# Causal attention on one core: each head's scores as two products of bfloat16 pieces, not three

## The chip, the cores and the metric

The kernel runs on one core of one Trainium2 chip. The metric is the device time of an execution in microseconds (us). TensorE (PE) multiplies matrices and writes its results to PSUM, a memory of eight banks here used in pieces of 128 partitions by 512 float32 numbers; VectorE (DVE) and ScalarE (ACT) read PSUM and SBUF; GpSimd (POOL) works on SBUF; SyncE (SP) issues most of the transfers. Each engine has its own queue, and semaphores hold an instruction until what it reads is there.

## The reference, cut to what matters

The program is a chain of four stages over one sequence of 2048 tokens of 128 features: a state-space layer, a layer of eight experts, causal attention with 16 heads of 8 features, and six layers of windowed attention with a gated network. Only the third is changed:

```python
scaling = D ** (-0.5)                       # D = 8
qkv = x @ W_qkv + b_qkv
q, k, v = jnp.split(qkv, 3, axis=-1)        # 16 heads each
scores = jnp.einsum('bhqd,bhkd->bhqk', q, k) * scaling
scores = jnp.where(mask[None, None, :, :], scores, -jnp.inf)    # causal
probs = jax.nn.softmax(scores, axis=-1)
out = jnp.einsum('bhqk,bhkd->bhqd', probs, v)
return out.transpose(0, 2, 1, 3).reshape(b, t, c) @ W_o + b_o
```

## The kernel before

**Pieces.** Scores are made by bfloat16 matmuls, and to keep nearly float32's precision, q and k are cut into bfloat16 pieces: the first piece is the rounded number, the next one the rounded rest, and so on. A head has 8 features, but its rows on TensorE are a strip of 32 partitions, in four slots of 8. Four heads form a group (`grp`, four groups), one strip each. The host lays out the weights (`_layouts`: `wqk`, `bqk`) so that the projection writes the same 8 features into the first three slots. The tile `kT` (`[P, NGRP, T]`) holds the first, second and third piece of k in those slots (`keys`), and constants of one in the first three rows of the fourth. The tile `q` (name `qT3`, `[P, 3, GW]`) holds one piece of q in each of its three planes, repeated over the slots (`project`). A product of plane i with kT is therefore one piece of q times all pieces of k; three products, summed in PSUM, make a score. Rows of the fourth slot of q's first plane take minus the row maximum, again in pieces, which the ones in kT add to each score.

**keys.** One call of the generator's step, for one group and 512 rows (a chunk `g`): PE projects into `pk`; ACT writes `one` (tile k0, shown as k) from it; DVE makes `krest`, the rest; POOL multiplies krest by a mask into `two` (tile k1, also shown as k) and subtracts it into kT. There are 16 calls: group 0 in `keys_values`, groups 1 to 3 in `keys`, for each of the four chunks. Buffers of one, two and krest rotate over two.

**project.** One call for each of 16 blocks (a group and 512 queries): PE projects into `pq`; ACT writes the first plane of q, DVE makes `qrest`, POOL casts it into the second plane and subtracts into the third. It is called a block ahead.

**Two passes.** For each block, `maxima` makes the scores with queries on the partitions and DVE takes their row maxima (`mx`, then `m`), which POOL splits (`m_piece`, `nm`) and PE transposes back (`ptm`) into the first plane of q. `attend` makes the scores again with keys on the partitions, ACT takes exp (`ex`), POOL zeroes the upper triangle of the diagonal tiles (an affine select on `ex`), and PE weighs the values (`av`). In the trace the products of maxima are sc<-kT,qT, those of attend sc<-qT,kT.

**The order.** Every instruction is pinned behind the one before it on its engine (`InOrder`), so the order of the program is that of each queue. `attention` interleaves the two passes: a unit of maxima (`part` of up to 512 keys, four heads) and a unit of attend (one tile of 128 keys, four heads) are taken together in two halves; each half has two heads of each pass:

```python
for half in range(2):
    m_heads, rest = step_m(ahead, half)
    heads, exps = part(1 - half)
    products(m_heads + heads)
    exps()
    weigh_due()
```

`products` runs over the pieces outside and the four heads inside, so that four strips of TensorE work at a time. `wanted` sets where units of one pass run alone. Scores and all other PSUM tiles of this stage take turns in seven banks (`psum_s`), the weighed values take the eighth.

**The beginning.** `front` gives each of the jobs (the end of the first stage, `experts`, `keys_values`, `keys`, and the attention's start) a due time, and `Merge` interleaves their steps by these times. Keys of the later chunks so stand among experts and halves of the attention: on ACT, for instance, after keys comes whatever step is due next, such as an exp.

Of the kernel before, what the change touches and what calls it, by code (L numbers as in the profile page):

```python
# [12 lines left out]
F32 = mybir.dt.float32  # L13
BF16 = mybir.dt.bfloat16
I32 = mybir.dt.int32
AF = mybir.ActivationFunctionType
ALU = mybir.AluOpType
# [3 lines left out]
P = 128  # L21
T = 2048
# [3 lines left out]
GW = G * P  # L26
# [6 lines left out]
HD1 = P // HEADS1  # L33
NGRP = 4
# [60 lines left out]
class Kernel:  # L95
# [102 lines left out]
    def load3(self, w):  # L198
        nc, a = self.nc, self.a
        wqk = w.tile([P, 2, NGRP, P], F32, name="wqk")  # L200
        nc.sync.dma_start(wqk, a["wqk1"])
        bqk = w.tile([P, 4, NGRP], F32, name="bqk")
        nc.sync.dma_start(bqk, a["bqk1"])
        wv = w.tile([P, P], F32, name="wv1")
        nc.sync.dma_start(wv, a["L1_attn_W_qkv"][:, 2 * P : 3 * P])
        wo = w.tile([P, P], F32, name="wo1")
        nc.sync.dma_start(wo, a["L1_attn_W_o"])
        self.w3 = wqk, bqk, wv, wo
# [259 lines left out]
    def keys(self, split, psum, g, hT3, kT, grps):  # L468
        wqk, bqk, wv, wo = self.w3
        hg = hT3[:, g * GW : (g + 1) * GW]  # L470
        for grp in grps:
            pk = psum.tile([P, GW], F32, name="pk", tag="b")
            self.pe.matmul(pk, lhsT=wqk[:, 1, grp, :], rhs=hg, start=True, stop=True)

            one, two = (split.tile([P, GW], BF16, name=f"k{i}") for i in range(2))
            rest = split.tile([P, GW], F32, name="krest")
            self.act.activation(
                one, pk, AF.Identity, bias=bqk[:, 2, grp : grp + 1], scale=bqk[:, 3, 0:1]
            )
            self.dve.scalar_tensor_tensor(rest, pk, bqk[:, 1, grp : grp + 1], one, ALU.add, ALU.subtract)  # L480
            self.gps.tensor_scalar_mul(two, rest, bqk[:, 3, 1:2])
            self.gps.tensor_tensor(kT[:, grp, g * GW : (g + 1) * GW], rest, two, ALU.subtract)
            yield 0.9

    def front(self, ctx, merge, psum, kvpool, x, hT3, kf, make_kT, va, xsT):
# [68 lines left out]
    def stages123(self, x, x3):  # L554
        nc, tc, a = self.nc, self.tc, self.a
        with ExitStack() as ctx:
            keep = ctx.enter_context(tc.tile_pool(name="s3keep", bufs=1))
            pool = ctx.enter_context(tc.tile_pool(name="s3", bufs=2))
# [3 lines left out]
            pe, dve, act, gps = self.pe, self.dve, self.act, self.gps  # L562
# [6 lines left out]
            wqk, bqk, wv, wo = self.w3  # L569
            hT = keep.tile([P, T], F32, name="hT3")  # L570
            kf = keep.tile([P, NGRP * T], F32, name="kf", tag="kT3")
            make_kT = lambda: keep.tile([P, NGRP, T], BF16, name="kT3", tag="kT3")
            va = keep.tile([P, NT, HEADS1, 32], F32, name="va")
            nms = [keep.tile([P, G, P], F32, name=f"nm{i}") for i in range(2)]
            xsT = keep.tile([P, T], F32, name="xsT", tag="ao")
# [2 lines left out]
            wait, kT = self.front(early, merge, banks, kvpool, x, hT, kf, make_kT, va, xsT)  # L578
# [23 lines left out]
            qs = {}  # L602
# [13 lines left out]

            def project(b):
                grp, qc = blocks[b]
                q = qs[b] = pool.tile([P, 3, GW], BF16, name="qT3", bufs=4)
                pq = bank("pq")  # L620
                pe.matmul(
                    pq, lhsT=wqk[:, 0, grp, :], rhs=hT[:, qc * GW : (qc + 1) * GW], start=True, stop=True
                )
                rest = pool.tile([P, GW], F32, name="qrest")
                act.activation(q[:, 0], pq, AF.Identity, bias=bqk[:, 0, grp : grp + 1])
                dve.scalar_tensor_tensor(rest, pq, bqk[:, 0, grp : grp + 1], q[:, 0], ALU.add, ALU.subtract)
                gps.tensor_copy(q[:, 1], rest)
                gps.tensor_tensor(q[:, 2], rest, q[:, 1], ALU.subtract)

            def products(heads):  # L630
                for i in range(3):
                    for product in heads:
                        product(i)


            def maxima(b):
                grp, qc = blocks[b]
                if b == 0:
                    project(b)
                q = qs[b]  # L640
                nm = nms[b % 2]
                m = pool.tile([P, G, 4], F32, name="m3")
                for j in range(G):
                    qt = G * qc + j
                    whole = (qt + 1) * P
                    chunks = [(c, min(GW, whole - c)) for c in range(0, whole, GW)]
                    mx = pool.tile([P, 4, NG], F32, name="mx3")

                    def part(pr, ch, qt=qt, mx=mx, chunks=chunks, j=j):
                        c, wd = chunks[ch]  # L650
                        n = len(chunks)
                        scs, heads = [], []
                        for h in (2 * pr, 2 * pr + 1):
                            sc = bank("sc1")
                            scs.append((h, sc))

                            def product(i, r=slice(32 * h, 32 * h + 32), sc=sc):
                                pe.matmul(
                                    sc[:, :wd], lhsT=q[r, i, j * P : (j + 1) * P], rhs=kT[r, grp, c : c + wd],
                                    start=i == 0, stop=i == 2 and ch < n - 1,  # L660
                                )

                            heads.append(product)

                        def rest():
                            for h, sc in scs:
                                if ch == n - 1:
                                    pe.matmul(sc[:, wd - P : wd], lhsT=self.ident16, rhs=mask, start=False, stop=True)
                                dve.reduce_max(mx[:, h, ch : ch + 1], sc[:, :wd], axis=AX.X)
                            if pr and ch == n - 1:  # L670
                                dve.tensor_reduce(m[:, j, :], mx[:, :, 0:n], axis=AX.X, op=ALU.max, negate=True)
                                if j == G - 1:
                                    pieces_of(m, nm)

                        return heads, rest

                    for ch, (_, wd) in enumerate(chunks):
                        yield wd, part, ch
                        if j == 0 and ch == 0 and b + 1 < len(blocks):
                            project(b + 1)  # L680

                def finish():
                    pt = bank("ptm")
                    for j in range(G):
                        pe.transpose(pt[:, j * P : (j + 1) * P], nm[:, j, :], self.ident)
                    dve.tensor_tensor(q[:, 0], q[:, 0], pt, ALU.add)

                yield 0, finish, None
# [14 lines left out]
            def attend(b):  # L703
                grp, qc = blocks[b]
# [14 lines left out]
                for kt in range(last + 1):  # L719
# [3 lines left out]
                    def part(pr, kt=kt, lo=lo):  # L723
                        nonlocal ex
                        if ex is None:
                            ex = pp.tile([P, 4, GW], F32, name="ex3")
                        scs, heads = [], []
                        for h in (2 * pr, 2 * pr + 1):
                            sc = bank("sc2")
                            scs.append((h, sc))  # L730

                            def product(i, r=slice(32 * h, 32 * h + 32), sc=sc):
                                pe.matmul(
                                    sc[:, lo:], lhsT=kT[r, grp, kt * P : (kt + 1) * P],
                                    rhs=q[r, i, lo:], start=i == 0, stop=i == 2,
                                )

                            heads.append(product)

                        def rest():  # L740
                            for h, sc in scs:
                                act.activation(ex[:, h, lo:], sc[:, lo:], AF.Exp)

                        return heads, rest
# [805 lines left out]
def _layouts(x):  # L1550

    f = np.float32
# [13 lines left out]
    got["bg"] = x["L0_ffn_bg"].reshape(1, P)  # L1566
    wqk = np.zeros((P, 2, NGRP, 4, 32), f)

    bqk = np.zeros((4, NGRP, 4, 32), f)
    for i in range(3):  # L1570
        s = slice(i * HD1, (i + 1) * HD1)
        wqk[..., s] = x["L1_attn_W_qkv"][:, : 2 * P].reshape(P, 2, NGRP, 4, HD1)
        bqk[0:2, ..., s] = x["L1_attn_b_qkv"][: 2 * P].reshape(2, NGRP, 4, HD1)
        if i:
            bqk[2, ..., s] = bqk[1, ..., s]
            bqk[3, 0, :, s] = 1.0
    bqk[3, 1, :, 2 * HD1 : 3 * HD1] = 1.0
    bqk[1, ..., 3 * HD1 : 3 * HD1 + 3] = 1.0
    got["wqk1"] = wqk.reshape(P, 2, NGRP, P)
    got["bqk1"] = bqk.reshape(4, NGRP, P).transpose(2, 0, 1)  # L1580
    got["bv1"] = x["L1_attn_b_qkv"][2 * P :].reshape(1, P)
    got["bo1"] = x["L1_attn_b_o"].reshape(1, P)
    swap = lambda s: np.concatenate([s[:, HD // 2 :], s[:, : HD // 2]], axis=1)
# [32 lines left out]
```

## Time and profile before

| | us |
|---|---|
| median of 3 runs (2319.01 to 2319.07) | 2319.02 |
| profiled execution | 2321.57 |
| its span, first to last instruction | 2319.6 |
| changed part: first keys to last scores | about 141 to 785 |

The profile is of one execution. A row of a group gives line, engine, operation, tiles (out<-in), shapes and count, then busy time, mean ns of one instruction, idle time of the engine before them and what ended it. A row of the timeline or of the chain of waits starts with the start in us and the duration. Every operation of this kernel is issued by one line of a helper (L67), so tiles and not lines tell them apart. The chain of waits follows the work that ended last back from the end, at each step to what released it.

### The profile page before, as it was taken

The numbers are of one execution on the slowest core, as the hardware profiler recorded it, in microseconds if no ns is written. First come the engines' busy times: TensorE is split into PE (matmuls) and PEld (weight loads), VectorE is DVE, ScalarE is ACT, GpSimd is POOL, SyncE is SP. The second block draws the span as 40 slices with busy tenths as digits, with TensorE's granted clock in tenths as the row PEclk, the third lists the DMA queues.
The fourth block names the chain that finished last, engine by engine and source line by source line (L and its number), as shares of the span: only waits on it lengthen the run. The fifth ranks groups of instructions, "written<-read, shape, count | busy, mean of one in ns | idle before, by whom it ended". The sixth has DMA issues, their size and how long they took to land.

```text
span 2319.6 us, 62002 instructions
## 1 busy us (share of the span) xinstructions
PE 2128.0 (92%) x26188; PEld 1233.9 (53%) x26188; DVE 1874.4 (81%) x2808; ACT 1638.1 (71%) x3219; POOL 1391.5 (60%) x2122
## 2 busy tenths in 40 slices
PE   4777988999999779999999999999999999999997
PEld 2654323333333346666666666666666666666654
DVE  6667677777766489999899988998999899998963
ACT  3322445566656578888888888888888888888881
POOL 4235411100011489988788878887888887887850
PEclk8787989999999979999999999999999999999998
DMA  2000000000000100000000000000000000000000
GB/s 78 1 1 1 2 2 2 2 2 2 2 2 2 68 2 20 4 20 2 20 11 23 2 20 11 22 2 20 11 22 2 20 9 3 2 2 2 2 6 14
DMA packets 14135, 25.38 MB, mean 11 GB/s; under 512 B 1657, under 2 KB 10530, under 8 KB 13090
## 3 DMA queue, kind: packets, MB, share of 16 engines
q1 hardware_dynamic: 13276, 20.97, 2.8%
q8 instruction: 206, 3.38, 0.6%
q14 instruction: 71, 0.58, 0.1%
q10 hardware_dynamic: 582, 0.46, 0.1%
HBM read 20.37 MB, written 1.05 MB: 9 GB/s over the span
## 4 chain that ended last, share of the span: by engine, by line
PE 64%; DVE 19%; ACT 8%; issue 4%; POOL 3%; DMA 0%; DVEq 0%; POOLq 0%; ACTq 0%; SPq 0%
PE big L67 45%; PE sc L67 9%; PE av L67 5%; DVE mx L67 4%; DVE rot_a L67 3%; DVE rot_b L67 2%; ACT sq L67 2%; ACT L67 1%; ACT ge L67 1%; DVE at L67 1%; ACT zs L67 1%; PE py L67 1%; ACT ex L67 1%; DVE act L67 1%; DVE ss L67 1%
## 5 line engine op out<-in xcount | busy, mean ns | idle before, releaser
L67 ACT ACTIVATE sm<-sm,mx,rn 128x64 f32<-128x64 f32 x1536 | 519.2, 430 | 0.3
L67 DVE TENSOR_REDUCE mx<-sc 128x1 f32<-128x512 f32 (+3 forms) x640 | 355.0, 604 | 125.5 <-PE sc L67 118.6
L67 POOL TENSOR_TENSOR rot_a<-rot_a,rot_b 128x1024 f32<-128x1024 f32 x192 | 454.6, 2368 | 0.1
L67 ACT ACTIVATE ex<-sc 128x512 f32<-128x512 f32 (+3 forms) x640 | 302.6, 536 | 204.1 <-PE sc L67 200.8
L67 PE MATMUL big<-wqk,s 128*128 128x512 f32 x768 | 369.2, 604 | 15.0 <-DVE rot_b L67 10.2
L67 PE MATMUL big<-zs,vo 128*128 128x256 f32 x1536 | 366.9, 382 | 0.3 <-ACT zs L67 0.3
L67 PEld LDWEIGHTS big<-zs,vo 128*128 128x128 f32 x1536 | 280.6, 190 | 88.3 <-issue 56.8
L67 DVE TENSOR_TENSOR rot_a<-big,tab 128x1024 f32<-128x1024 f32 x192 | 233.5, 1216 | 47.1 <-ACT sq L67 36.4
L67 PE MATMUL sc<-qT,kT 32*128 32x512 bf16 (+3 forms) x1920 | 248.4, 351 | 24.6 <-DVE mx L67 16.3
L67 ACT ACTIVATE sq<-big 128x1024 f32<-128x1024 f32 x192 | 197.4, 1028 | 76.0 <-PE big L67 46.1
L67 ACT COPY zs<-big 128x1024 f32<-128x1024 f32 x192 | 192.3, 1006 | 64.3 <-PE big L67 64.3
L67 PE MATMUL sc<-kT,qT 32*128 32x512 bf16 (+3 forms) x1920 | 232.4, 359 | 1.6 <-DVE krest L67 0.5
L67 DVE TENSOR_REDUCE ss<-sq 128x16 f32<-128x1024 f32 x192 | 229.8, 1198 | 1.4
L67 DVE TENSOR_TENSOR rot_b<-big,tab 128x1024 f32<-128x1024 f32 x192 | 230.0, 1198 | 0.3 <-POOL rot_a L67 0.3
L67 PE MATMUL big<-at,xw 32*128 32x512 f32 x1536 | 206.2, 624 | 3.9 <-DVE rot_b L67 1.7
L67 PEld LDWEIGHTS big<-wqk,s 128*128 128x128 f32 x768 | 135.7, 192 | 137.0 <-issue 125.6
L67 PE MATMUL big<-ident,rot_a 128*128 128x128 f32 x1536 | 198.9, 276 | 6.2 <-POOL rot_a L67 3.6
L67 PEld LDWEIGHTS big<-ident,rot_a 128*128 128x128 f32 x1536 | 176.6, 142 | 50.3 <-issue 23.5
L67 POOL TENSOR_SCALAR_AFFINE_SELECT ex<-ex 128x512 f32<-128x512 f32 x64 | 40.8, 638 | 269.8 <-ACT ex L67 269.6
L67 POOL TENSOR_TENSOR sm<-sm,su 128x1024 f32<-128x1024 f32 x96 | 183.1, 1907 | 23.4 <-DVE su L67 22.2
L67 PE MATMUL av<-ex,va 128*32 128x256 f32 (+1 forms) x2432 | 180.5, 377 | 5.0 <-POOL ex L67 3.7
L67 POOL TENSOR_TENSOR rot_a<-rot_a,rn 128x1024 f32<-128x1024 f32 x96 | 182.7, 1904 | 0.2
(236 smaller groups left out, 3342.4 us busy)
## 6 DMA issues: line engine op xcount, KB each, us to landing
wqk<-in_L_ffn_Wqkv SPq DMA_DIRECT2D x12, 512.0 KB, 4.9
wvo<-in_wvo SPq DMA_DIRECT2D x6, 1024.0 KB, 4.9
w<-in_L_ffn_W SPq DMA_DIRECT2D x6, 341.0 KB, 7.5
x<-in_L_attn_hidden_states SPq DMA_DIRECT2D x4, 256.0 KB, 4.3
out<-act SPq DMA_DIRECT2D x4, 256.0 KB, 2.3
rot<-in_rot SPq DMA_DIRECT2D x1, 960.0 KB, 7.0
w<-in_L_ffn_W SPq DMA_DIRECT2D x12, 64.0 KB, 1.9
qks<-in_qks SPq DMA_DIRECT2D x6, 128.0 KB
```

Of the source, the lines that this page charges most:

```text
L67: return self._tc.keep_in_program_order(call(*args, **kw))
```

## The change

q now has two planes and kT two. Plane 1 of kT is the old kT (three pieces of k in three slots) but with k's first piece in the fourth slot instead of the constants of one; plane 0 is made from it by one more ACT instruction that multiplies by a mask (first three slots) and adds a bias (the ones in the fourth slot). Plane 0 of q is q's first piece in three slots, made by one more ACT instruction from a tile `one`; plane 1 holds q's second piece in three slots and its third piece in the fourth, made on POOL: a multiply by a mask into `two` and a subtraction. The products with index 0 and 1 then contain what the three contained, but for the third piece of q, which meets only the first piece of k.

```diff
     def load3(self, w):
-        bqk = w.tile([P, 4, NGRP], F32, name="bqk")
+        bqk = w.tile([P, 5, NGRP], F32, name="bqk")
     def keys(self, split, psum, g, hT3, kT, grps):
             self.dve.scalar_tensor_tensor(rest, pk, bqk[:, 1, grp : grp + 1], one, ALU.add, ALU.subtract)
             self.gps.tensor_scalar_mul(two, rest, bqk[:, 3, 1:2])
-            self.gps.tensor_tensor(kT[:, grp, g * GW : (g + 1) * GW], rest, two, ALU.subtract)
+            cols = slice(g * GW, (g + 1) * GW)
+            self.gps.tensor_tensor(kT[:, 1, grp, cols], rest, two, ALU.subtract)
+            self.act.activation(
+                kT[:, 0, grp, cols], kT[:, 1, grp, cols], AF.Identity, bias=bqk[:, 3, 3:4], scale=bqk[:, 3, 2:3]
+            )
             yield 0.9
     def stages123(self, x, x3):
-            make_kT = lambda: keep.tile([P, NGRP, T], BF16, name="kT3", tag="kT3")
+            make_kT = lambda: keep.tile([P, 2, NGRP, T], BF16, name="kT3", tag="kT3")
             def project(b):
-                q = qs[b] = pool.tile([P, 3, GW], BF16, name="qT3", bufs=4)
+                q = qs[b] = pool.tile([P, 2, GW], BF16, name="qT3", bufs=4)
...
-                act.activation(q[:, 0], pq, AF.Identity, bias=bqk[:, 0, grp : grp + 1])
-                dve.scalar_tensor_tensor(rest, pq, bqk[:, 0, grp : grp + 1], q[:, 0], ALU.add, ALU.subtract)
-                gps.tensor_copy(q[:, 1], rest)
-                gps.tensor_tensor(q[:, 2], rest, q[:, 1], ALU.subtract)
+                one, two = (pool.tile([P, GW], BF16, name=f"q{i}") for i in range(2))
+                act.activation(one, pq, AF.Identity, bias=bqk[:, 0, grp : grp + 1])
+                dve.scalar_tensor_tensor(rest, pq, bqk[:, 0, grp : grp + 1], one, ALU.add, ALU.subtract)
+                act.activation(q[:, 0], one, AF.Copy, scale=bqk[:, 3, 2:3])
+                gps.tensor_scalar_mul(two, rest, bqk[:, 4, 0:1])
+                gps.tensor_tensor(q[:, 1], rest, two, ALU.subtract)
             def products(heads):
-                for i in range(3):
+                for i in range(2):
                     for product in heads:
                         product(i)
```

In both passes the product of index i now takes plane i of kT (`kT[r, i, grp, ...]` in place of `kT[r, grp, ...]`) and the last index is 1 and not 2. The host's layout fills the fourth slot of `wqk` and `bqk` too, and adds the masks: row 3 of `bqk` gets entries 2 (first three slots) and 3 (ones of the fourth), row 4 a mask of the fourth slot.

More of the change, by code (lines that the diff above doesn't have):

```diff
@@ L658, in product @@
                                 pe.matmul(
-                                    sc[:, :wd], lhsT=q[r, i, j * P : (j + 1) * P], rhs=kT[r, grp, c : c + wd],
-                                    start=i == 0, stop=i == 2 and ch < n - 1,
+                                    sc[:, :wd], lhsT=q[r, i, j * P : (j + 1) * P], rhs=kT[r, i, grp, c : c + wd],
+                                    start=i == 0, stop=i == 1 and ch < n - 1,
                                 )
@@ L733, in product @@
                                 pe.matmul(
-                                    sc[:, lo:], lhsT=kT[r, grp, kt * P : (kt + 1) * P],
-                                    rhs=q[r, i, lo:], start=i == 0, stop=i == 2,
+                                    sc[:, lo:], lhsT=kT[r, i, grp, kt * P : (kt + 1) * P],
+                                    rhs=q[r, i, lo:], start=i == 0, stop=i == 1,
                                 )
@@ L1567, in _layouts @@
     wqk = np.zeros((P, 2, NGRP, 4, 32), f)
-    bqk = np.zeros((4, NGRP, 4, 32), f)
-    for i in range(3):
+    bqk = np.zeros((5, NGRP, 4, 32), f)
+    for i in range(4):
         s = slice(i * HD1, (i + 1) * HD1)
@@ L1573, in _layouts @@
         bqk[0:2, ..., s] = x["L1_attn_b_qkv"][: 2 * P].reshape(2, NGRP, 4, HD1)
-        if i:
+        if i in (1, 2):
             bqk[2, ..., s] = bqk[1, ..., s]
@@ L1577, in _layouts @@
     bqk[3, 1, :, 2 * HD1 : 3 * HD1] = 1.0
-    bqk[1, ..., 3 * HD1 : 3 * HD1 + 3] = 1.0
+    bqk[3, 2, :, : 3 * HD1] = 1.0
+    bqk[3, 3, :, 3 * HD1 : 3 * HD1 + 3] = 1.0
+    bqk[4, 0, :, 3 * HD1 :] = 1.0
     got["wqk1"] = wqk.reshape(P, 2, NGRP, P)
-    got["bqk1"] = bqk.reshape(4, NGRP, P).transpose(2, 0, 1)
+    got["bqk1"] = bqk.reshape(5, NGRP, P).transpose(2, 0, 1)
     got["bv1"] = x["L1_attn_b_qkv"][2 * P :].reshape(1, P)
```

## The prediction

> **What bounds the kernel now.** I read the page first, then the busy time by windows over the third stage (the changed code runs from 135 to 785 us), then the timeline of some of its halves, the chain of waits through its beginning, and the groups by shape. A measurement here can tell about 0.2%, some 4.6 us, from no change; "same" means within that.
>
> ```profile
> PE 2128.0 (92%) x26188; PEld 1233.9 (53%) x26188; DVE 1874.4 (81%) x2808; ACT 1638.1 (71%) x3219; POOL 1391.5 (60%) x2122
> 135.00:300.00 165.00, 135.30 (x1237) 71.17 (x1236) 112.38 (x273) 57.41 (x133) 77.97 (x99) 0.86 0.00 1
> 300.00:785.00 485.00, 440.78 (x5768) 158.75 (x5769) 335.15 (x653) 288.33 (x596) 63.58 (x143) 0.97 0.02 6
> ```
> The window rows give, after the length, PE, PEld, DVE, ACT and POOL, then the granted clock. From 300 on PE is busy for 441 of 485 us, DVE for 335, ACT for 288: TensorE leads, VectorE is not far behind. Before 300 nothing is full; order and latency decide. In both parts the engines take the order in which the program names its instructions.
>
> ```profile
> 559.73 0.23 PE L67 MATMUL sc<-kT,qT 32*128 32x128 bf16 x2
> 560.49 0.64 PE L67 MATMUL av<-ex,va 128*32 128x256 f32 x8
> 566.57 0.39 PE L67 MATMUL sc<-kT,qT 32*128 32x512 bf16 x2
> 566.79 0.38 PE L67 MATMUL sc<-kT,qT 32*128 32x512 bf16 x2
> 567.01 0.38 PE L67 MATMUL sc<-kT,qT 32*128 32x512 bf16 x2
> 567.38 0.64 PE L67 MATMUL av<-ex,va 128*32 128x256 f32 x8
> 567.42 2.68 DVE L67 TENSOR_REDUCE mx<-sc 128x1 f32<-128x512 f32 x4 [0.23 <-PE sc L67]
> 568.90 0.64 PE L67 MATMUL av<-ex,va 128*32 128x256 f32 x8
> 570.29 0.64 PE L67 MATMUL av<-ex,va 128*32 128x256 f32 x8
> ```
> This timeline is the unit of the stage, a half: twelve products (three rounds of four heads), then eight weighing matmuls (av). Rounds follow each other at 0.22 us (566.57, 566.79, 567.01). A half without a wait goes from first product to first av in 0.76 us (559.73 to 560.49). From 567.38 to 570.29 two halves take 2.91 us while four reductions keep DVE for 2.68 of it, idle for 0.23 before them: here DVE is nearly the bound.
>
> ```profile
> 141.03 0.75 ACT k L67
> 141.81 0.77 DVE krest L67
> 142.67 1.58 POOL k L67
> 144.32 1.15 POOL kT L67
> 145.48 1.56 POOL k L67
> 147.11 1.16 POOL kT L67
> 148.30 0.75 DVE krest L67
> 149.05 1.20 DVE own L67 x2
> ```
> This is the chain of waits through the keys of the first 512 rows. Four keys calls (one for each group of heads) follow each other there, and the chain runs through them: POOL hands out one kT each 2.79 us (142.67 to 145.46 or 145.48), and behind the last krest (148.30) stand the experts' instructions on DVE (own). The chain runs likewise through the keys at 169 to 176, 198, 209 to 219, 237 and 257 to 261 us.
>
> **The products removed.** Each head's score goes from three products to two, one round of 0.22 us per half. By the code's schedule 126 units carry a maximum part and an attend part (two halves each), 34 a maximum part alone and 34 an attend part alone (one pass of four heads each). The widest head of every half and pass sums to 152,448 columns; at 0.215 us per 512 that is 64 us, the end of the range if TensorE alone set the pace. The other end is near zero: the reductions stay, and 448 of them are 512 wide.
> I go by the bursts of products after 300 us, from first product to what PE does next: 77 take 0.70 to 0.765 us (no wait), 20 less (narrow), 78 take 0.77 to 1.0, 76 longer (134.9 us in all), those mostly waiting for DVE. The first gain the whole round, 77 x 0.215 = 16.6 us; the narrow ones 20 x 0.1 = 2. The third kind falls to DVE's pace, (2.91 - 2.68)/2 = 0.11 us each: 78 x 0.11 = 8.6. Of the last I give a quarter of a round, 76 x 0.05 = 4, since a run of reductions that already fills DVE ends when it ends. With 3 us for the part before 300: **34 us gained**, bounds 18 and 50.
>
> **The projection of q.** Each of 16 calls gets one more ACT instruction (q[:, 0] from one) and a POOL multiply by a per-partition mask in place of the cast.
> ```profile
> L67 POOL TENSOR_SCALAR k<-krest,bqk 128x512 bf16<-128x512 f32 x16 | 25.1, 1567 | 21.6 <-DVE krest L67 21.6
> L67 POOL CAST qT<-qrest 128x512 bf16<-128x512 f32 x16 | 9.8, 612 | 41.5 <-DVE qrest L67 41.2 <-PE sc L67 0.3
> ```
> The same form of multiply takes 1567 ns in keys, the cast 612: +0.955 us on POOL, in front of the masks of the diagonal scores (ex, affine select). Those already arrive late: at 552.86 PE waits 0.41 us for POOL ex, directly behind the projection's two instructions. In about eight of the 16 calls a mask follows directly: 8 x 0.955 = **8 us lost**; bounds 0 (all covered) and 16 x 0.955 = 15. The extra ACT step waits for nothing that is late; ACT is busy for 59% after 300 and I count it at nothing; uncovered it costs 16 x 0.7 = 11.
> The Trainium skill, "GPSIMD Engine Reference", Engine selection, calls one-input work on this engine roughly line-rate, which would make both instructions alike and this term 0, and the total 8 us lower; the two rows above, 1567 and 612 ns on the same shape, speak against that.
>
> **The keys, where I expect the loss.** kT now has two planes. POOL writes plane 1; then ACT makes plane 0 from it, in the same step of the program. No row shows an ACT operation on bf16 from SBUF of this size; nearest are kT<-kT,carry (128x256, SBUF, 511 ns) and k<-pk,bqk (128x512, 779 ns): bounds 0.51 and 0.78, I take 0.7, nearer the second for its width. What counts is the wait. ACT's order is fixed, so the new instruction holds ACT until POOL is done, and behind it stands the next keys call's first instruction (k), for which DVE's krest waits, for which all of DVE's queue waits. One keys call then follows the other at 0.78 (k) + 0.75 (krest) + 1.57 + 1.15 (POOL) + 0.7 + some 0.35 for the five hand-overs (0.03 to 0.1 each in the chain) = 5.3 us, not 2.79.
> - Keys at 141 to 148: first krest 141.81, fourth now 148.30, then 141.81 + 3 x 5.3 = 157.7: **+9.4**. What is late next: own, then py on PE, both on the chain.
> - Keys at 169 to 176: likewise 169.05 + 15.9 against 175.52: **+9.4**.
> - Keys at 198 (one call): ACT's next work is at 205.62, after 8.46 us idle, and the new step would end at about 202: nothing.
> - Keys at 209 to 216 (three calls, between halves of the attention): the exps of two halves (2.16 us) stand between the second and third k, so krest moves from 215.89 to 209.49 + 10.6 + 2.2, and the scores' seven PSUM banks stay taken until the exps have run: 6 to 9, I take **8**.
> - One call at 235: the four exps behind it move from 235.84 to the end of kT and the new step, 240.6; seven banks let PE run on for a while: **3** (0 to 5).
> - Keys at 256 to 261 (three calls, a q projection between): the third krest moves from about 261.5 to 257.11 + 10.6 + 2.7 for q's longer steps, and the exps at 261.01 come behind all three, at about 274: 9 to 13, I take **12**.
> Sum **42 us lost**. If half of it were covered, 21; with every exp waiting, 50.
>
> **The clock.** While ACT waits, PE runs dry. In the trace the granted clock is already 0.86 over 135 to 300, and the same pair of pk matmuls takes 1.08 us at 213.90 and 2.07 at 254.19. I add two such doublings, **2 us** (0 to 10).
> The skill's "TensorE: Matmul & The Clock Gate", Part 1, says that an idle window of about 3.4 us halves TensorE's clock and that as long a busy one is needed to restore it; estimated from that page, some nine new gaps would cost up to 1.7 us each, 15 us instead of 2, and the total would be 13 us higher.
>
> The rest has one answer: the longer bqk load (20 instead of 16 numbers per partition) lies under the load of x; q's buffers shrink and one and two take their place; kT's planes fill the space kf leaves. 0.
>
> **Sum.** -34 + 8 + 42 + 2 = +18 us. The profiled execution took 2321.57 us (span 2319.6 and 1.97 around it), 2.55 over the median of the runs; so 2339.6 by its own time, and 2337 as a median.
>
> **Rivals.**
> - The keys' waits are covered, and it gets faster. If merged work lets DVE and PE run on while ACT waits, the front costs little and -34 + 8 = -26 remains: 2293. For it: PE idles 30 of 165 us there, so work is at hand. Against it: the chain runs through krest at each of these places, and the queues don't change order. It decides from 26 us, a mean wait of 1.9 us more per call over 14 calls. Chance 0.19.
> - DVE becomes the bound throughout: the rounds save only 16 us, q's longer POOL steps cost 15, the rest stays: -16 + 15 + 42 + 2 = +43, 2362. For it: the 76 bursts that already wait. Against it: DVE idles 150 of 485 us. Chance 0.2.
> - The shorter bursts bring nothing because something else paces a half: the third round would then vanish without av coming earlier. The spacing of 0.22 in rows of unhindered halves speaks against it; with it +52, 2371. Chance 0.04.
> My forecast, a front loss over the gain, has the rest, 0.57; its own range is 2318 to 2355.
>
> **Range and chances.** 2300 to 2362 leaves out most of the first rival and the last. Faster by over 0.2%: the first rival and a little of the forecast, 0.21; within 0.2%: the forecast's low end, 0.10; slower 0.69.
>
> **What would show it.** Right: ACT idle before kT with POOL kT as releaser, over 35 us in 16 waits; the first sc products some 19 us later than 190.6; unhindered halves at 0.54 us; in the steady blocks (affine selects at 499.8, 552.2 and 604.5 now, 52.4 us apart) a spacing of 48 to 50; POOL's q multiply at 1.57. Wrong: kT waits under 1 us, or krest still paced by POOL, or a block spacing under 46.5.

## The result and the profile after

The kernel after takes 2325.75 us (median of 12 runs, 2323.39 to 2329.88) where the kernel before, run beside it, takes 2319.05: the ratio is 1.0025, 95% interval 1.0016 to 1.0034, so some 6 us slower. The forecast was slower, by 18. The profiled execution of after took 2329.88 us (span 2328.0), 8.3 over that of before.

Placed by landmarks of the two traces: the seventh projection of q (pq6), which stands just behind the last key of the front, starts at 285.55 us before and at 327.05 after, 41.5 later. The last ex ends at 781.51 and at 791.73, so 31.3 of that were regained in the attention. The rest of the program gave 1.8 more, so the traces show 8.5 us; the profiled executions lie 4.1 (after) and 2.5 (before) above their medians, which differ by 6.7. A small sum of two large terms, then, as forecast; one of the two was mis-sized.

The page's engine line, and two of its groups:

```profile
PE 2092.3 (90%) x24908; PEld 1199.1 (52%) x24908; DVE 1865.9 (80%) x2808; ACT 1660.2 (71%) x3251; POOL 1403.7 (60%) x2122
...
L67 DVE TENSOR_REDUCE mx<-sc 128x1 f32<-128x512 f32 (+3 forms) x640 | 348.9, 604 | 111.5 <-PE sc L67 110.5
...
L67 PE MATMUL av<-ex,va 128*32 128x256 f32 (+1 forms) x2432 | 187.5, 390 | 11.5 <-POOL ex L67 9.9
```

PE has 1280 instructions fewer and ACT 32 more, as the diff says. The same two groups on the page of before:

```profile
L67 DVE TENSOR_REDUCE mx<-sc 128x1 f32<-128x512 f32 (+3 forms) x640 | 355.0, 604 | 125.5 <-PE sc L67 118.6
...
L67 PE MATMUL av<-ex,va 128*32 128x256 f32 (+1 forms) x2432 | 180.5, 377 | 5.0 <-POOL ex L67 3.7
```

The row of av is the price on POOL: before, av waited 3.7 us for the masked ex, now 9.9. The row of mx shows that DVE still idles 110 us for scores, 119 before.

The busy time by windows over the front and the attention of after (length, PE, PEld, DVE, ACT, POOL, granted clock):

```profile
135.00:300.00 165.00, 105.43 (x677) 55.21 (x680) 82.30 (x210) 51.60 (x105) 74.47 (x82) 0.74 0.00 1
327.00:795.00 468.00, 412.45 (x4836) 132.68 (x4835) 339.38 (x679) 303.34 (x624) 75.10 (x146) 0.93 0.02 6
```

In the same first 165 us PE now does 677 matmuls where it did 1237, at a clock of 0.74 where it had 0.86. No engine there is busier than before; that the order makes it late is shown below (x1_plane_later).

The front, in the waits of after from 135 to 330 us (who waited for whom; us in all, times, longest), and in the chain through the first keys:

```profile
ACT kT L67 <- POOL kT L67: 63.5, 16, 5.1
...
DVE krest L67 <- ACT k L67: 40.8, 13, 5.9
...
POOL k L67 <- DVE krest L67: 37.5, 12, 7.8
```

```profile
140.80 0.76 DVE krest L67
...
141.66 1.58 POOL k L67
...
143.32 1.16 POOL kT L67
...
144.50 0.81 ACT kT L67
145.31 0.67 ACT k L67
...
146.01 0.76 DVE krest L67
```

The first list is a ring: ACT waits for POOL's kT, DVE for ACT's k, POOL for DVE's krest. The chain goes round it once per key: krest at 140.80 and again at 146.01, 5.2 us later (forecast 5.3; 2.79 before).

In the attention, the steady blocks. These are POOL's masks on the timeline of after:

```profile
527.39 1.23 POOL L67 TENSOR_SCALAR_AFFINE_SELECT ex<-ex 128x512 f32<-128x512 f32 x2
...
576.02 1.22 POOL L67 TENSOR_SCALAR_AFFINE_SELECT ex<-ex 128x512 f32<-128x512 f32 x2
...
625.20 1.23 POOL L67 TENSOR_SCALAR_AFFINE_SELECT ex<-ex 128x512 f32<-128x512 f32 x2
```

They are 48.6 and 49.2 apart, inside the 48 to 50 of the forecast. Some long bursts shrank by more than one round, though. The same burst of twelve products before (545.18) and of eight after (568.17), each in its timeline:

```profile
545.18 0.39 PE L67 MATMUL sc<-kT,qT 32*128 32x512 bf16 x2
...
545.32 2.67 DVE L67 TENSOR_REDUCE mx<-sc 128x1 f32<-128x512 f32 x4
...
546.05 0.32 PE L67 MATMUL sc<-qT,kT 32*128 32x384 bf16 x1 [0.48 <-DVE mx L67]
...
546.63 0.64 PE L67 MATMUL av<-ex,va 128*32 128x256 f32 x8
```

```profile
568.17 0.39 PE L67 MATMUL sc<-kT,qT 32*128 32x512 bf16 x2
...
568.62 0.34 PE L67 MATMUL sc<-qT,kT 32*128 32x384 bf16 x2
...
568.88 0.64 PE L67 MATMUL av<-ex,va 128*32 128x256 f32 x8
```

From first product to av it took 1.45 us and now takes 0.71: 0.74 saved by leaving out a round of 0.22. The other half microsecond is the wait for DVE (0.48 at 546.05), which is gone. Elsewhere it isn't. At 481.24 before and at 509.66 after, again in one and the same burst, the wait has grown by what the round took:

```profile
481.24 0.37 PE L67 MATMUL sc<-qT,kT 32*128 32x512 bf16 x1 [0.21 <-DVE mx L67]
```

```profile
509.66 0.37 PE L67 MATMUL sc<-qT,kT 32*128 32x512 bf16 x1 [0.42 <-DVE mx L67]
```

Both times this burst takes 1.33 us.

### The profile page after: what moved, and what is told of

Read it like the earlier page. It is cut to its first block, busy times and chain, and to the rows that moved or that the text cites. A ratio compares the mean times of both kernels' runs of the same rounds, so it can differ in the third digit from the quotient of the medians.

```text
span 2328.0 us, 59452 instructions
## 1 busy us (share of the span) xinstructions
PE 2092.3 (90%) x24908; PEld 1199.1 (52%) x24908; DVE 1865.9 (80%) x2808; ACT 1660.2 (71%) x3251; POOL 1403.7 (60%) x2122
## 4 chain that ended last, share of the span: by engine, by line
PE 60%; DVE 20%; ACT 9%; issue 5%; POOL 5%; DMA 0%; DVEq 0%; POOLq 0%; ACTq 0%; SPq 0%
PE big L67 44%; PE sc L67 6%; DVE mx L67 5%; PE av L67 5%; DVE rot_a L67 3%; DVE rot_b L67 2%; ACT sq L67 2%; ACT ex L67 1%; ACT L67 1%; ACT ge L67 1%; DVE at L67 1%; PE py L67 1%; ACT zs L67 1%; DVE ss L67 1%; DVE act L67 1%
## 5 line engine op out<-in xcount | busy, mean ns | idle before, releaser
L67 DVE TENSOR_REDUCE mx<-sc 128x1 f32<-128x512 f32 (+3 forms) x640 | 348.9, 604 | 111.5 <-PE sc L67 110.5
L67 PE MATMUL sc<-qT,kT 32*128 32x512 bf16 (+3 forms) x1280 | 205.3, 372 | 36.8 <-DVE mx L67 15.5
L67 PE MATMUL av<-ex,va 128*32 128x256 f32 (+1 forms) x2432 | 187.5, 390 | 11.5 <-POOL ex L67 9.9
L67 PE MATMUL sc<-kT,qT 32*128 32x512 bf16 (+3 forms) x1280 | 190.0, 375 | 5.8 <-DVE krest L67 1.8
```

Source lines behind the costliest of these rows:

```text
L67: return self._tc.keep_in_program_order(call(*args, **kw))
```

## The experiments

My theory: the front costs some 42 us because ACT waits at the head of its order; the rounds save more than I gave them; q's longer POOL step costs what I gave it or more. The rivals: POOL's own chain sets the front's pace; DVE bounds the gain; POOL's step is covered. All times are medians, all ratios against the kernel before run on the same chip, with 95% intervals. To compare kernels measured at different times I multiply differences of ratios by 2319 us; such a difference carries about 3 to 5 us of uncertainty.

### Each part alone

The rounds alone, from the kernel before:

```diff
-                for i in range(3):
+                for i in range(2):
                     for product in heads:
```

(with `stop` at index 1.) Expected:

> The kernel before with two rounds of score products in place of three: the product of the third piece of q is left out, so the scores are less exact; the third piece is still made. It is the gain of the change by itself. Theory (bursts measured in the two traces, 47 us shorter after pq6 with the change): 38 to 50 us faster than before, 2269 to 2281. My forecast's term: 31 to 34 faster, 2285 to 2288. Rival (DVE's maxima bound the attention, the products are hidden beside them): under 20 us faster, over 2299.

Measured: 2278.02 us, ratio 0.9827 (0.9813 to 0.984), so 40 us faster, as the bursts of the trace said. From pq6 to the last ex its trace takes 448.8 us, before 496.0. DVE doesn't bound the gain as that rival had it; with the same reductions to make, it now idles less for scores than the 118.6 us of before:

```profile
L67 DVE TENSOR_REDUCE mx<-sc 128x1 f32<-128x512 f32 (+3 forms) x640 | 348.1, 602 | 90.7 <-PE sc L67 89.9
```

The keys' extra ACT step alone, from the kernel before:

```diff
-            self.gps.tensor_tensor(kT[:, grp, g * GW : (g + 1) * GW], rest, two, ALU.subtract)
+            cols = slice(g * GW, (g + 1) * GW)
+            self.gps.tensor_tensor(kT[:, 1, grp, cols], rest, two, ALU.subtract)
+            self.act.activation(
+                kT[:, 0, grp, cols], kT[:, 1, grp, cols], AF.Identity, bias=bqk[:, 3, 1:2], scale=bqk[:, 3, 0:1]
+            )
```

> The kernel before with the front's part of the change alone: POOL's last step writes plane 1 of a kT of two planes, ACT writes plane 0 from it in the same place of its order as in the kernel after, and nobody reads plane 0; three rounds and q's steps as before. It is the price of the wait by itself. Theory: 35 to 45 us slower than before, 2354 to 2364, with pq6 near 327 (before 285.6). Rival (the front of the kernel after is late for its colder clock or for something that q's steps bring): under 15 us slower.

Measured: 2364.61 us, ratio 1.0202 (1.0189 to 1.0215), 47 us slower, a little over the range. pq6 starts at 329.43, and the attention behind it takes 496.5 us, as before: the whole loss of the trace lies in the front. The wait in its list:

```profile
ACT kT L67 <- POOL kT L67: 62.2, 16, 5.0
```

The longer POOL step of q alone, from the kernel before:

```diff
-                gps.tensor_copy(q[:, 1], rest)
+                gps.tensor_scalar_mul(q[:, 1], rest, va[:, 0, 0, HD1 : HD1 + 1])
```

> The kernel before with POOL's cast of q's rest (612 ns) replaced by a multiply by a per-partition column of ones (about 1565 ns), the same values: the price of q's longer POOL step by itself, 16 times. Theory (the masks and the pieces of q queue behind it): 6 to 12 us slower than before, 2325 to 2331, with more first products of av waiting for POOL's ex. Rival 1 (hidden, one-input work is as quick): within 3 us of before. Rival 2 (each late mask also puts TensorE to half clock for a while): 13 us slower or more. If x2, x3 and x4 add up, their sum should be near the change's own +6.7 us.

Measured: 2332.02 us, ratio 1.0066 (1.0054 to 1.0078), 15 us slower: over the theory's range and in that of the second rival, but its reason doesn't hold, since the granted clock from 288 to 791 us is the 0.97 of before. Instead, PE waits for masks, 7.8 us more than the 3.7 of before. Its group on the page:

```profile
L67 PE MATMUL av<-ex,va 128*32 128x256 f32 (+1 forms) x2432 | 182.8, 382 | 12.9 <-POOL ex L67 11.5
```

Those 7.8 us are about what its trace loses behind pq6: 503.2 us from pq6 to the last ex in place of 496.0. pq6 itself comes 2.7 later. The traced executions differ by 9.9 of the 15; the rest is not located.

The three alone give -40 + 47 + 15 = +22, not the change's +6. They do not add.

### Each loss taken out of the kernel after

Plane 0 later, so that ACT takes the next key first:

```diff
-            self.act.activation(
-                kT[:, 0, grp, cols], kT[:, 1, grp, cols], AF.Identity, bias=bqk[:, 3, 3:4], scale=bqk[:, 3, 2:3]
-            )
+            self.merge.add(4.0, self.plane(kT, grp, cols))
             yield 0.9
```

(`plane` is a generator that issues that one instruction; `front` sets `self.merge`.)

> The kernel after, with ACT's new step for plane 0 of kT put into the order 4 units of the planner later as a job of its own, so that ACT takes the next keys' step first; nothing else is changed. Theory (ACT, waiting on POOL at the head of its order, sets the front's key period): the 16 waits of ACT for kT on POOL (63.5 us in the kernel after) fall under 25 us, pq6 starts near 290 to 300 (before 285.6, after 327.1), and the time is 25 to 40 us below after: 2286 to 2301. Rival 1 (POOL's own chain of two steps for each key sets the period, and ACT only shows it): pq6 stays later than 318 and the time is within 8 us of after, 2318 to 2334. Rival 2 (what the front gives back is lost in the attention, where another limit holds): pq6 comes early, the time is still over 2310.

Measured: 2295.28 us, ratio 0.9905 (0.989 to 0.9919): 30 us below after by the medians, 28 by the ratios. pq6 starts at 289.37; the wait is down to a quarter:

```profile
ACT kT L67 <- POOL kT L67: 15.5, 9, 2.0
```

This decides the front. The instruction takes ACT 810 ns, in after 813; where it stands in ACT's order was worth some 28 us. POOL's chain (rival 1) doesn't set the period, and the attention (rival 2) keeps what it is given: 467.4 us from pq6 to the last ex, in after 464.7. The colder clock is no cause of the late front either: from 135 us to pq6 it is 0.72 in after, but also 0.77 here and 0.75 with the rounds alone, where pq6 starts at 288.28.

The long POOL step taken out in two ways, by a plain cast and by ACT:

```diff
-                gps.tensor_scalar_mul(two, rest, bqk[:, 4, 0:1])
+                gps.tensor_copy(two, rest)
```

> The kernel after with a plain cast in place of the masked multiply on POOL; the mask over the rows of the second piece is left out, so the scores are not exact. It takes the long step away without giving ACT anything. Theory: 12 to 18 us faster than after, 2308 to 2314, and as quick as or quicker than with the multiply on ACT. Rival (some other step of q's chain, such as ACT's second step for each block, holds the attention): within 5 us of after.

```diff
-                gps.tensor_scalar_mul(two, rest, bqk[:, 4, 0:1])
+                act.activation(two, rest, AF.Copy, scale=bqk[:, 4, 0:1])
```

> The kernel after with q's masked multiply made by ACT (one more step on ACT for each of 16 blocks) in place of POOL; keys as in the kernel after. Theory (q's long POOL step of 1.57 us holds up the masks behind it, and with only two rounds nothing covers that): 10 to 17 us faster than after, 2309 to 2316, waits of av for POOL's ex falling. Rival (it was covered, or ACT's step takes its place): within 4 us of after, 2322 to 2330.

Measured: 2319.81 us, ratio 0.9992 (0.9981 to 1.0003), with the cast, and 2321.55, ratio 1.0002 (0.999 to 1.0013), on ACT: 8 and 5 us better than after by the ratios. That is under the theory's ranges, which took the 15 of the step alone, and just over the rivals'. The intervals lie clear of that of after, so the step has a price, but with 3 to 5 us of uncertainty the size is rough: about the 8 of the forecast in the whole change.

### Do they overlap?

Rounds with the long POOL step, from the kernel before (both diffs above):

> The kernel before with two rounds (the third piece's product left out) and POOL's multiply by ones in place of its cast for q: whether the long POOL step costs more beside two rounds than beside three, where it cost 14.5 us. Theory (the blocks are shorter, and less covers the masks): 16 us or more over the two rounds alone, 2294 or more, with the stretch from pq6 to the last ex near the 467 us of the kernel after and of the one with plane 0 later (two rounds alone 449, before 496). Rival (it adds as it is, and something else of the change takes the difference): 2288 to 2293. Rival (the longer step is covered): under 2283.

Measured: 2290.81 us, ratio 0.9869 (0.9848 to 0.9891): 10 us over the rounds alone by the ratios, so my theory of a dearer step was wrong, and the first rival, that it simply adds, is nearer. Its trace does have 468.4 us from pq6 to the last ex, as the theory had it, but that execution took 2298.01, the slowest of its runs.

The plane with the long POOL step, and the plane with two rounds, both from the kernel before:

> The kernel before with the keys' extra ACT step in its waiting place and with q's longer POOL step, but with three rounds as before: do the two prices add? Alone they cost 47 and 15 us. Theory (in the front ACT's wait covers what the long step costs there, about 5.6 us between pq5 and pq6 with the step alone; only the 7 to 10 us of the attention are left): 2370 to 2376, and pq5 to pq6 takes 41 to 43 us. Rival (they add): 2378 to 2384, pq5 to pq6 over 46.

> The kernel before with the keys' extra ACT step in its waiting place and two rounds of products (the third piece's product left out), q's steps as before. Alone they were worth +47 and -40 us. Theory (fewer products in the front take nothing from its key chain, but the rounds save more once the chain has delayed the attention, so that the two overlap): 2314 to 2321. Rival (they add): 2323 to 2330.

Measured: 2371.02 us, ratio 1.0225 (1.0211 to 1.0239), and 2318.15 us, ratio 0.9993 (0.9982 to 1.0005). Both times fall in the theory's ranges: the parts overlap. The place I gave for the first was wrong: pq5 to pq6 takes 45.7 us with both, 41.9 with the plane alone, so 3.8 of the step's 5.6 us there are not covered. The time fell into the range by luck; where the two overlap is not shown. All ratios together, in us of 2319:

| part | alone | beside the long POOL step | beside the plane | beside two rounds | beside both others |
|---|---|---|---|---|---|
| two rounds | -40 | -46 | -48 | | -46 |
| plane 0 in its waiting place | +47 | +37 | | +38 | +36 |
| long POOL step | +15 | | +5 | +10 | +8 |

The last column compares the kernel after with x9_plane_multiply, x7_rounds_multiply and x8_cast. After and x8_cast also hold ACT's second step of q, which the others lack; x8_cast and x10_plane_rounds differ in it and have the same ratio within 0.0001, so it costs nothing that shows here. Each loss is dearest alone, and the gain is largest in company. Why the plane's price falls from 47 to 37 is not shown: in single traces, which differ by a few us from execution to execution, it moves pq6 by 43.9 us alone, 42.4 beside two rounds, 46.3 beside the long step and 37.6 beside both, which isn't the order of the times.

### Versions that beat both

Both repairs together, plane 0 later and the masked multiply on ACT; and the same with plane 0 on DVE:

```diff
-        self.act.activation(
-            kT[:, 0, grp, cols], kT[:, 1, grp, cols], AF.Identity, bias=bqk[:, 3, 3:4], scale=bqk[:, 3, 2:3]
-        )
+        self.dve.tensor_scalar(
+            kT[:, 0, grp, cols], kT[:, 1, grp, cols], bqk[:, 3, 2:3], bqk[:, 3, 3:4], ALU.mult, ALU.add
+        )
```

> The kernel after with both repairs: ACT's plane 0 of kT 4 units later, and q's masked multiply on ACT. Theory: the two add, 41 to 47 us faster than after and near the two rounds alone, 2279 to 2285. Rival (the two repairs load ACT, which then ends last): over 2290.

> The kernel after with plane 0 of kT made by DVE, 4 planner units later, and q's masked multiply on ACT: a candidate, against the one with both steps on ACT (2281.7). Theory (ACT is free of the plane in the front; DVE's step from bfloat16 in SBUF is short): pq6 near 288 and 2275 to 2282. Rival (DVE, waiting on POOL at the head of its order, holds up its own work): over 2287.

Measured: 2281.73 us, ratio 0.9833 (0.981 to 0.9857), and 2281.12 us, ratio 0.9839 (0.9826 to 0.9852). Both are some 38 us faster than the kernel before and 43 to 45 faster than after, and about as quick as the rounds alone: the idea of the change is worth its 40 us when its two side steps are moved. On DVE the plane takes 568 ns in the mean (median 404, longest 1379) and ACT is free of it, but the time doesn't show that. pq6 starts at 292.04 there, not near 288.

## Why the prediction was right or wrong

**The keys: right.** Forecast 42, by places; in the traces:

| landmark | forecast, summed | measured |
|---|---|---|
| fourth key | 9.4 | 8.2 |
| eighth | 18.8 | 16.8 |
| ninth | 18.8 | 16.4 |
| thirteenth | 26.8 | 23.3 |
| fourteenth | 29.8 | 27.6 |
| pq6, behind the last | 41.8 | 41.5 |

The measured column holds whatever else of the change falls in the front. The earlier places cost a little less than forecast and the last one more (13.9 where it had 12). By times, x3_plane_alone gave 47, and the same part beside the others 36. ACT's new step takes 813 ns, not 0.7 us, and outside the bounds of 0.51 and 0.78; over 16 steps that is 2 us.

**The products: the step that failed.** The mechanism, a round less in each burst, was right; the term of the long bursts was mis-sized, 4 us where it measured 25. I pair the bursts of products of before and after in their order, from pq6 to the last ex, by what they took before (259; the forecast counted 251 from 300 us):

| before, us | bursts | forecast | saved in after | saved by the rounds alone |
|---|---|---|---|---|
| 0.70 to 0.765 | 80 | 16.6 | 14.0 | 16.0 |
| under 0.70 | 22 | 2 | 1.1 | 0.9 |
| 0.765 to 1.0 | 79 | 8.6 | 7.3 | 8.1 |
| longer | 78 | 4 | 25.2 | 27.6 |

Three terms of four were right to within 2.6 us. The fourth, "I give a quarter of a round ... since a run of reductions that already fills DVE ends when it ends", missed by 21. Its 78 bursts are of several kinds.

- 21 hold 24 products and not 12, because two units follow each other without an av between, so that two rounds fall away. They saved 5.4 us in after. The trace of before could have told that.
- The other 57 saved 19.8. Of these, 21 saved nothing, like the one at 481.24: the forecast's reason holds for them, and PE's recorded waits for mx in them grew from 1.7 to 3.7 us.
- Another 21 saved 13.0, which is 0.62 each and far more than a round of 0.22, like the one at 545.18. PE's waits for mx in them fell from 5.3 to 1.6 us. My reading: DVE had been late at these places because it had itself waited for products; when the bursts ahead get shorter, the reductions start earlier, and the wait at the long burst shrinks too. DVE's idle time for sc over the two bursts ahead fits it (36.8 us, then 27.8), that over the last one hardly does (11.8, then 11.1), and no run isolates it.
- 8 saved 1.6.
- 7 saved 5.5 for another reason: they ran at half clock before, wholly or in part, and at full clock in after and with the rounds alone. Six of them follow each other from 320.75 on, with their rounds about 0.42 apart and no recorded wait inside. The window of before (granted clock 0.53):

```profile
320.00:334.00 14.00, 13.91 (x133) 3.95 (x136) 7.33 (x15) 4.07 (x13) 2.57 (x4) 0.53 0.01 2
```

The forecast took its 76 bursts mostly for waits for DVE; in 33 of them the trace records no such wait. In the others a wait for DVE was taken for a sign that DVE is full, which holds for some of them only. Half clock at these six bursts stands in the traces of before and x4_q_multiply, in part in that of x3_plane_alone, and not in that of x9_plane_multiply, all with three rounds; its cause is not shown. By times the term is -40 alone and -46 in company, where the sum had -34.

**q's steps: right in size.** Forecast 8, by the ratios 8 in the whole change (x8_cast against after, 3 to 5 us of uncertainty); 15 alone, at the upper bound. The multiply takes 1566 ns in after. The Trainium skill's rule ("GPSIMD Engine Reference", Engine selection, one-input work roughly at line rate) would have made it 0; x4_q_multiply, where only the form of the one-input step changes, speaks against that.

**The sum.** Forecast -34 + 8 + 42 + 2 = +18. In the traces, the front lost 41.5. In the attention the bursts of products saved 47.5, the bursts of av lost 13.7 (159.1 to 172.8 us; 165.5 with the cast, so about half of it is the long POOL step, and some 5 us come with the rounds alone) and the rest 2.5; behind the attention 1.8 were saved. Together that is +8.5. Against the forecast's terms it is 13.5 us more from the products, 6 more lost to av and the rest than the 8 and the 2, and 2 less in the front (0.5) and behind the attention (1.8): the 9.5 us between +18 and the traces' +8.5. (The 34 counted 3 us before 300, which here lie in the front's 41.5.) The miss of the products alone is larger than that of the sum; av took part of it back, so that by luck the sum is better than its terms. The 2 us for the clock are part of av's.

**The rivals.** Covered waits (2293) fell with the 63.5 us of ACT kT; DVE as the bound (2362) fell with the rounds alone; products that bring nothing (2371) likewise. Of the signs named ahead, the 16 waits (63.5 us), the step of 1.57, the spacing and the halves at 0.54 (0.51 to 0.57 at 360 to 366 us) came as said; the first scores came 16.4 later (190.58 to 207.02), not 19.

## What to carry to other kernels

An instruction that waits for another engine costs what stands behind it in its queue, not its own duration: put it where its input is already there (here some 28 us for one line moved by a few steps). A wait for an engine that itself idles elsewhere need not be a bound; ask what that engine waited for before, since the wait can go when its feeder gets faster (here at 21 bursts of 57, while at 21 others nothing was gained). Look at the clock before a long burst is put down to a wait. Count the instructions inside a unit before a saving per unit is multiplied, and measure parts of a change in company as well as alone: here the three alone gave +22, together +6.

## What the runs showed of the hardware

TensorE's clock fell to half without any long stop. On the timeline of after, a mask that comes late behind q's long step (576.02, above) holds PE for 1.44 us; and the windows around it (length, PE, PEld, DVE, ACT, POOL, clock):

```profile
576.71 0.43 PE L67 MATMUL av<-ex,va 128*32 128x128 f32 x8 [1.44 <-POOL ex L67]
```

```profile
573.90:577.30 3.40, 1.84 (x37) 0.64 (x32) 1.66 (x3) 1.43 (x6) 3.26 (x4) 1.00 0.00 0
577.30:580.70 3.40, 3.40 (x36) 1.08 (x29) 0.75 (x2) 2.68 (x6) 0.00 (x0) 0.50 0.02 5
```

PE was busy for 1.84 of 3.4 us, and the next 3.4 ran at half clock. The same block before had 2.99 busy of 3.4 (549.4 to 552.8) and stayed at 1.00. But such a wait doesn't decide by itself. One block earlier in after, PE waits as long for the same mask, and the clock stays at 1.00:

```profile
528.08 0.42 PE L67 MATMUL av<-ex,va 128*32 128x128 f32 x8 [1.45 <-POOL ex L67]
```

```profile
525.00:532.00 7.00, 5.20 (x81) 1.84 (x80) 3.52 (x7) 4.31 (x12) 3.53 (x4) 1.00 0.00 0
```

From pq6 to the last ex the clock is 0.93 in the three kernels that have two rounds and the long POOL step (after, x1_plane_later, x7_rounds_multiply), 0.98 with the rounds alone, 0.96 with the cast in place of the long step, and 0.97 and 0.98 with the long step beside three rounds (x4_q_multiply, x9_plane_multiply). The low clock stands only where both come together; that the waits for masks bring it is argued, not shown. The Trainium skill, "TensorE: Matmul & The Clock Gate", Part 1, speaks of an idle window of about 3.4 us; the length of the step agrees, but here the clock also fell after a window of that length in which PE was busy for more than half of it. How much of the av bursts' 13.7 us is this and how much the masks was not separated.
